# Weaving VectorE's dependent chains in the first pass of a two-layer graph and mixture-of-experts kernel

## The chip, the cores and the metric

The kernel runs on one core of one Trainium2 chip. The metric is the device time of one execution in microseconds, as the median of some runs. A kernel has five engines that matter here: TensorE (PE in the profile, with its weight loads shown as PEld), VectorE (DVE), ScalarE (ACT), GpSimd (POOL) and SyncE (SP). Each runs its own list of instructions in order and waits on semaphores for the others. SP and POOL issue most of the DMAs.

## The reference

There are 128 graphs of 64 nodes with 256 features, 8192 tokens in all, in float32. Two layers follow each other, and each is a graph part and a mixture-of-experts part, with a residual around each of them:

```python
# layer 0
x = x + gnn0(layernorm(x), adj)     # agg = eps*x + adj@x; h = silu(rmsnorm(agg@W1 + b1)); h@W2 + b2
x = x + ffn0(layernorm(x))          # 64 experts, top 6, see below
# layer 1
x = x + gnn1(layernorm(x), adj)     # h = layernorm(x); x + relu((adj@h)@W_rel + b_rel + h@W_root)
x = x + ffn1(layernorm(x))          # 8 experts, top 2, 256 -> 512 -> 256 with relu

def ffn0(x):
    top, idx = top_k(x @ gate_w.T, 6)
    lattice_out = sum_k softmax(top)[k] * (x @ lattice_weights[idx[k]])
    return layernorm(x + lattice_out @ out_w.T + out_b)
```

## The kernel before, in words

The tokens are handled in NB = 32 blocks of C = 256, each of T = 2 tiles of 128 tokens. There are four stretches of work, one after the other.

The first pass (to about 610 us) computes the first graph part and the routing to the 64 experts. It is a software pipeline: `staggered(n, stages)` runs a list of pairs (lag, function), and in step s it calls each function for block s - lag. The list is written by hand, and since PE, DVE and ACT are scheduled by hand, it is also the order of the instructions on these engines. In one step block s gets its hidden layer (`hidden`, 32 matmul records of L716; ScalarE squares them into `sq`, L719), the sum of squares by three halving additions (`square_sum`, L726), the root mean square (`rms`, L730 on TensorE) and the scaling (`scale`: eight times L738 on VectorE and a silu on ScalarE, L740). Block s + 1 gets its statistics and its norm (`norm_a`, L45 and L46; `norm_s`; `norm_b`, L698) and the aggregation over its neighbours (`aggregate`, L706, copied out by ScalarE, L709). Block s - 1 gets the second matrix (`project`, L747 and L749). Block s - 2 gets the residual, its statistics and the layer norm (`residual_a`, `residual_s`, `residual_b`), the transposition (`turn`, L89) and the gate logits (`gate`, L784). Block s - 3 is routed.

Routing is the class `Router`. `choosing` finds the eight largest logits (L217), their indices (L220), and compares the first K = 6 indices with the numbers of the experts (L226), which gives K one-hots per token. `count` multiplies them with a triangle and with ones on TensorE (L240), once for each rank, so that each token gets its position among the tokens of its expert. `placing` adds the running counts (L343 to L354), multiplies with the one-hots (L356) and sums over the experts (L359): the row of each copy of a token in a table in DRAM. `weigh`, `normalize` and `release` make the softmax weights (L306 to L328). `send` writes the six copies of a block's rows to the table by twelve indirect DMAs of GpSimd (L369). `books` are small updates of the chunks of the table's space, in turn over four blocks (`keep_books`). The normed rows go into `xs`, of which there are three buffers; `residual_b` also stores x1 and the normed rows (`xn1_dram`, L771) for the third pass.

The second pass (about 640 to 1150 us) loads the pages of the table in turn, multiplies them with the lattice of their expert, and GpSimd writes the answers back by indirect DMAs (L376).

The third pass (about 1110 to 1520 us) is again a staggered list. It loads the answers (`load_y`), x1 and the normed rows (`load3`, L1107 and L1109), computes the output of the first mixture part (`output`, whose first instruction is L1158, the sum of the projection and the normed rows), the second graph part (L1222 to L1245) and the second routing, with its own `xs` (L1259, three buffers; L315 is GpSimd's write of the destinations into it). Here the VectorE chains are already generators which take turns: `chain` makes from a generator a function that carries it on by one `yield`. Some pages of the second mixture are worked on between the blocks (`up`, L1048, and `down`).

The last stretch runs the pages of the second mixture, L1048 and L1059 on TensorE.

Of the kernel before, what the change touches and what calls it, by code (L numbers as in the profile page):

```python
# [27 lines left out]
class Ops:  # L28
# [55 lines left out]
    def transpose(self, pt, x):  # L84

        n = x.shape[1]
        for k in range(2):
            for t in range(n):
                self.nc.tensor.transpose(pt[:, k, ts(t, P)], x[:, t, ts(k, P)], self.ident)  # L89


class Router:
# [91 lines left out]
    def iota(self, shape, pattern, m, name):  # L184
        t = self.pool.tile(shape, F32, name=self.name + name)
        i = self.small.tile([P, 384], I32, name="iota", bufs=1)[:, :t.free_size()]
        if len(shape) == 3:
            i = i.rearrange("p (a b) -> p a b", b=shape[2])
        self.nc.gpsimd.iota(i, pattern=pattern, base=0, channel_multiplier=m)
        self.nc.vector.tensor_copy(t, i)  # L190
        return t

    def begin(self, counts, work, psum):
# [3 lines left out]
        self.nc.vector.tensor_copy(self.run[:, 0, :], self.base)  # L197

# [12 lines left out]
    def choosing(self, logits, B):  # L211
# [7 lines left out]
        for t in range(T):  # L219
            nc.vector.max_index(idx[:, t, :], top[:, t, :], logits[:, t, :])  # L220
            yield
        which = self.small.tile([P, T, K], F32, name=n + "which")
        nc.vector.tensor_copy(which, idx[:, :, :K])
        yield
        B["hot"] = hot = self.work.tile([P, T, K, E], BF16, name=n + "hot")
        nc.vector.tensor_tensor(hot, self.expert.unsqueeze(1).unsqueeze(1).to_broadcast([P, T, K, E]),  # L226
                                which.unsqueeze(3).to_broadcast([P, T, K, E]), op=ALU.is_equal)
        yield

    def choose(self, logits):  # L230
        B = {}
        for _ in self.choosing(logits, B):
            pass
        return B["top"], B["hot"]

    def count(self, hot):

        for m, lhsT in enumerate((self.tri, self.ones)):
            for k in range(self.K):
                self.nc.tensor.matmul(self.psum[:, m], lhsT=lhsT, rhs=hot[:, :, k, :],  # L240
                                      start=(k == 0), stop=(k == self.K - 1))

    def books(self):
# [5 lines left out]
        def reach_a():  # L249

            v.tensor_tensor(new, run(), self.end, op=ALU.is_ge)
            v.tensor_mul(t, new, self.delta)
            v.tensor_add(run(), run(), t)
            v.tensor_add(self.base, self.base, t)

        def reach_b():
            v.scalar_tensor_tensor(t, new, S, t, op0=ALU.mult, op1=ALU.add)
            v.tensor_add(self.end, self.end, t)
            v.tensor_add(self.none, self.none, new)

        def grow_a():

            v.tensor_sub(t, self.end, run())
            v.scalar_tensor_tensor(new, t, float(self.EP), self.none, op0=ALU.is_lt, op1=ALU.mult)
            v.tensor_tensor_scan(cum, new, self.zero[:, :E], self.used, op0=ALU.add, op1=ALU.add)
            v.tensor_copy(self.used, cum[:, E - 1:E])
            v.tensor_scalar(cum, cum, -1.0, float(self.pitch), op0=ALU.add, op1=ALU.mult)

        def grow_b():
            v.tensor_sub(t, cum, self.end)  # L270
            v.tensor_sub(t, t, self.delta)
            v.tensor_mul(t, t, new)
            v.tensor_add(self.delta, self.delta, t)
            v.tensor_sub(self.none, self.none, new)

        def note_a():

            v.scalar_tensor_tensor(cum, self.alloc, -S, cum, op0=ALU.mult, op1=ALU.add)
            v.tensor_mul(cum, cum, new)

        def note_b():
            self.hit = self.work.tile([P, self.J, E], F32, name=n + "hit", bufs=1)
            v.tensor_tensor(self.hit, self.nth, self.alloc.unsqueeze(1).to_broadcast([P, self.J, E]), op=ALU.is_equal)

        def note_c():
            v.tensor_mul(self.hit, self.hit, cum.unsqueeze(1).to_broadcast([P, self.J, E]))

        def note_d():
            v.tensor_add(self.map, self.map, self.hit)
            v.tensor_add(self.alloc, self.alloc, new)  # L290

        return (reach_a, reach_b), (grow_a, grow_b), (note_a, note_b), (note_c, note_d)

    def keep_books(self, b, half):

        if self.J > 1 and b >= self.epoch:
            if b % self.epoch == 0 and half == 0:
                self.todo = self.books()
            self.todo[b % self.epoch][half]()
# [21 lines left out]
    def normalize(self, w, den):  # L321
        nc = self.nc
        nc.vector.reduce_sum(den, w, axis=AX.X)
        nc.vector.reciprocal(den, den)

# [3 lines left out]

    def places(self, b, hot):  # L330
        B = {"hot": hot}
        for _ in self.placing(B):
            pass
        return B["row"]

    def placing(self, B):
# [13 lines left out]
        if self.J > 1:  # L350
            over = self.work.tile([P, T, E], F32, name=n + "over", bufs=1)
            nc.vector.tensor_tensor(over, place, self.end.unsqueeze(1).to_broadcast([P, T, E]), op=ALU.is_ge)
            nc.vector.tensor_mul(over, over, self.delta.unsqueeze(1).to_broadcast([P, T, E]))
            nc.vector.tensor_add(place, place, over)  # L354
        prod = self.work.tile([P, T, K, E], F32, name=n + "prod", bufs=1)
        nc.vector.tensor_mul(prod, hot, place.unsqueeze(2).to_broadcast([P, T, K, E]))  # L356
# [173 lines left out]
def two_layer_gnn_moe_kernel(ctx: ExitStack, tc: tile.TileContext, a: dict, out: bass.AP):  # L530
# [84 lines left out]
    xn1_dram = [dram.tile([C, D], F32, name=f"xn1_{b}") for b in range(NB)]  # L615
# [21 lines left out]
    with tc.tile_pool(name="c0", bufs=1) as c0, \  # L637
# [23 lines left out]
        nc.scalar.dma_start(out=w1, in_=a["L0_gnn_W1"].rearrange("(k p) f -> p k f", p=P))  # L661
# [23 lines left out]

        def norm_e(b):
# [6 lines left out]
        def norm_b(b):  # L693
# [3 lines left out]
            for t in range(T):  # L697
                nc.vector.tensor_scalar(xn[:, t, :], x[:, t, :], mv[:, t, 0:1], rs[:, t:t + 1],  # L698
                                        op0=ALU.subtract, op1=ALU.mult)

# [21 lines left out]
        def square_sum(b):  # L722
            h = KH
            while h > 1:
                h //= 2
                nc.vector.tensor_add(sq[:, :h, :], sq[:, :h, :], sq[:, h:2 * h, :])  # L726

# [6 lines left out]
        def scale(b):  # L734
# [6 lines left out]
            nc.scalar.preload_act_table_set("natural_log_exp_and_others")  # L741
# [10 lines left out]
        def residual_a(b):  # L752
# [3 lines left out]
            B["mv1"] = ops.stats(x1)  # L756

        def residual_s(b):
            blocks[b]["rs1"] = ops.rstd(blocks[b]["mv1"][:, :, 1], 1e-5)

        def residual_b(b):
            B = blocks[b]
            x1, mv, rs = B["x1"], B["mv1"], B["rs1"]
# [7 lines left out]
            nc.sync.dma_start(out=by_tile(xn1_dram[b]), in_=xs[:, :, 0, :D])  # L771
# [15 lines left out]
        def choose(b):  # L787
            B = blocks[b]
            B["top"], B["hot"] = r0.choose(pg)
# [5 lines left out]
        def count(b):  # L795
            r0.count(blocks[b]["hot"])

        def place(b):
            B = blocks[b]
            r0.normalize(*B["w"])  # L800
            B["row"] = r0.places(b, B["hot"])
# [12 lines left out]
        def load_lattice(b):  # L814
# [10 lines left out]
        norm_b(0)  # L825
# [6 lines left out]
        r0.begin(counts, work, route)  # L832
        staggered(NB, (
            (3, choose),
            (3, lambda b: r0.keep_books(b, 0)),
            (2, residual_a),
            (4, lambda b: send(b, 2)),
            (-2, lambda b: load0(b) if b > 1 else None),
            (-1, rest(norm_a)),
            (0, lambda b: hidden(b, 0)),  # L840
            (0, lambda b: hidden(b, 1)),
            (2, residual_s),
            (-1, rest(norm_s)),
            (-1, rest(norm_e)),
            (4, lambda b: send(b, 3)),
            (3, weigh),
            (0, lambda b: hidden(b, 2)),
            (0, lambda b: hidden(b, 3)),
            (3, count),
            (2, residual_b),  # L850
            (-1, rest(norm_b)),
            (4, lambda b: send(b, 4)),
            (0, split_late),
            (1, lambda b: project(b, 0, 0, 4)),
            (3, lambda b: r0.keep_books(b, 1)),
            (4, lambda b: send(b, 5)),
            (0, square_sum),
# [3 lines left out]
            (2, turn),  # L861
            (0, rms),
            (3, place),
            (1, lambda b: project(b, 1, 0, KH)),
            (2, gate),
            (0, scale),
            (3, lambda b: send(b, 1)),
            (1, load_lattice),
# [170 lines left out]
    def up(i, lo=0, hi=KF):  # L1039
# [5 lines left out]
        for c in range(lo, hi):  # L1045
            ph = Q["ph"](c)
            for k in range(KD):
# [422 lines left out]
```

## Time and profile before

| | |
|---|---|
| runs, us | 2025.9, 2020.5, 2021.36; median 2021.36 |
| the profiled execution's own time, us | 2032.17 |
| its span, us | 2030.3 |
| granted TensorE clock, mean of the span | 0.98 |
| busy share of the span: PE, PEld, DVE, ACT, POOL | 93%, 81%, 58%, 50%, 58% |
| moved by DMA | 397.90 MB, 196 GB/s |

The span is from the first to the last instruction of one profiled execution; its own time is that of the same execution on the device. A row of the timeline has the start in us, the busy time in us, the engine, the line of the kernel, the operation with what it writes and reads, and the number of instructions merged into the row; behind it, in brackets, stands how long the engine sat idle before and what ended that. A row of the groups has the number of instructions, their busy time and the mean of one in ns, and the idle time before them. A row of the waits has who waited for whom, the total in us, how often and the longest.

### The profile page before, as it was taken

The page shows a single profiled execution, that of the slowest core. Times are in us where ns is not written, and L with a number is a line of the kernel's source. Part 1 is how long each engine was busy: PE and PEld are TensorE (multiplying, and loading weights), DVE is VectorE, ACT ScalarE, POOL GpSimd, SP SyncE. Part 2 cuts the span into 40 slices and gives each one's busy share as a digit, 9 for nine tenths or more (in the row PEclk, how much of TensorE's full clock was granted, in tenths as well). Part 3 has the DMA queues.
Part 4 walks back from the last instruction along what each step waited for, and adds up shares of the span by engine and source line. Part 5 has one row for each costly group of instructions (what it writes and reads, how often), then busy time and mean ns, then how long its engine had stood idle before and what let it go on. Part 6 is the DMA issues. An engine that isn't in the chain of part 4 may idle for free. (4 is left out here: it accounts for less than half of the span.)

```text
span 2030.3 us, 36761 instructions
## 1 busy us (share of the span) xinstructions
PE 1898.1 (93%) x10324; PEld 1648.7 (81%) x10324; DVE 1169.2 (58%) x4165; ACT 1012.5 (50%) x2033; POOL 1169.7 (58%) x1134
## 2 busy tenths in 40 slices
PE   6999999999966899999999799999989999999995
PEld 5888888888854777888877588788868888888885
DVE  5899999999975333343333378899852222222221
ACT  4888888888851222222222266666643333333331
POOL 1376667677677777777777734344444444444443
PEclk9999999999977999999999999999999999999998
DMA  4244555544486988766666889988527766766774
GB/s 117 86 143 151 169 166 175 171 157 147 136 264 202 310 259 262 216 206 207 209 208 184 310 311 302 321 305 303 170 89 190 173 162 160 168 157 162 162 162 87
DMA packets 282559, 397.90 MB, mean 196 GB/s; under 512 B 56024, under 2 KB 236392, under 8 KB 282352
## 3 DMA queue, kind: packets, MB, share of 16 engines
q1 hardware_dynamic: 202880, 246.61, 40.8%
q0 software_dynamic: 64416, 136.14, 22.3%
q10 hardware_dynamic: 15056, 12.69, 1.9%
q8 instruction: 93, 1.52, 0.3%
q14 instruction: 114, 0.93, 0.2%
HBM read 222.84 MB, written 176.64 MB: 197 GB/s over the span
## 5 line engine op out<-in xcount | busy, mean ns | idle before, releaser
L369 POOL DMA_INDIRECT r0x<-xs,r0row x384 | 396.5, 1033 | 230.2 <-issue 67.0
L376 POOL DMA_INDIRECT r0y<-px x404 | 393.2, 973 | 124.6 <-DMA r0y<-px 47.3
L974 PE MATMUL py<-lat,pxT 128*128 x1616 | 388.0, 383 | 18.7 <-ACT pxT L961 15.7
L386 POOL DMA_INDIRECT out_x<-py_s,px x138 | 215.3, 1560 | 291.0 <-DMA out_x<-py_s,px 216.2
L978 DVE TENSOR_SCALAR px<-py,px 128x256 f32<-128x256 f32 x404 | 177.0, 480 | 311.4 <-PE py L974 307.5
L974 PEld LDWEIGHTS py<-lat,pxT 128*128 128x128 f32 x1616 | 292.6, 191 | 59.7 <-ACT pxT L961 21.3
L961 ACT COPY pxT<-pt 128x512 f32<-128x512 f32 x202 | 118.1, 586 | 370.4 <-PE pt L959 251.0
L1050 ACT ACTIVATE phid<-ph,pw 128x256 f32<-128x256 f32 x264 | 125.2, 474 | 311.5 <-issue 167.0
L1059 PE MATMUL py<-fw,phid 128*128 (+1 forms) x1072 | 242.5, 379 | 0.1
L1048 PE MATMUL ph<-pxT,pw 128*128 128x256 f32 x1056 | 238.7, 379 | 0.0
L749 PE MATMUL ps<-lat 128*128 128x256 f32 x1024 | 238.5, 381 | 0.0
L716 PE MATMUL ph<-lat 128*128 128x256 f32 x1024 | 233.5, 387 | 2.7 <-DVE lat L738 2.0
L1048 PEld LDWEIGHTS ph<-pxT,pw 128*128 128x128 f32 x1056 | 200.6, 190 | 27.3
L716 PEld LDWEIGHTS ph<-lat 128*128 128x128 f32 x1024 | 196.1, 194 | 29.8 <-issue 2.4
L1059 PEld LDWEIGHTS py<-fw,phid 128*128 128x128 f32 x1072 | 198.5, 190 | 24.6 <-ACT phid L1050 0.3
L749 PEld LDWEIGHTS ps<-lat 128*128 128x128 f32 x1024 | 193.8, 192 | 24.9
L369 POOL DMA_INDIRECT r1x<-xs,r1row x128 | 136.9, 1070 | 76.0 <-ACT hn L1194 14.4
L959 PE MATMUL pt<-ident,px 128*128 128x128 f32 x808 | 126.0, 277 | 13.7 <-DMA px<-r0x 13.3
L1068 DVE TENSOR_SCALAR p<-p 128x2 f32<-128x2 f32 x69 | 11.7, 169 | 219.5 <-ACT p L1067 219.5
L1074 DVE TENSOR_TENSOR py_s<-py,pb 128x512 f32<-128x512 f32 x67 | 46.4, 692 | 152.6 <-PE py L1059 152.6
L959 PEld LDWEIGHTS pt<-ident,px 128*128 128x128 f32 x808 | 100.9, 142 | 40.1 <-issue 10.0
L719 ACT ACTIVATE lat<-ph,c_L_gnn_b 128x256 f32<-128x256 f32 x256 | 103.5, 471 | 13.6 <-PE ph L716 11.9
(322 smaller groups left out, 2951.1 us busy)
## 6 DMA issues: line engine op xcount, KB each, us to landing
px<-r0x SPq DMA_DIRECT2D x404, 129.0 KB
y<-r0y SPq DMA_DIRECT2D x64, 768.0 KB
pw<-in_L_ffn_W1b SPq DMA_DIRECT2D x69, 514.0 KB
px<-r1x SPq DMA_DIRECT2D x69, 258.0 KB
x<-x SPq DMA_DIRECT2D x64, 256.0 KB
pb<-in_L_ffn_b SPq DMA_DIRECT2D x69, 128.0 KB
r0x<-r0filler ACTq DMA_DIRECT2D x64, 129.0 KB
lat<-in_x SPq DMA_DIRECT2D x32, 256.0 KB
```

The lines of the kernel that those rows point to most:

```text
L369: i = self.nc.gpsimd.indirect_dma_start(out=self.table[:, :], out_offset=bass.IndirectOffsetOnAxis(ap=row[:, t, k:k + 1], axis=0), in_=xs[ ...
L376: d = self.nc.gpsimd.indirect_dma_start(out=self.answer[:, :], out_offset=bass.IndirectOffsetOnAxis(ap=x[:, self.D:self.D + 1].bitcast(I32 ...
L386: i, d = f"{self.name}add{i}", self.nc.gpsimd.indirect_dma_start(out=self.total[:, :], out_offset=bass.IndirectOffsetOnAxis(ap=x[:, self.D ...
L716: nc.tensor.matmul(ph[:, c, :], lhsT=w1[:, k, ts(2 * j + c, P)], rhs=B["aggT"][:, k, :], start=(k == 0), stop=(k == KD - 1))
L749: nc.tensor.matmul(B["po"][:, t, :], lhsT=B["hT"][:, c, ts(t, P)], rhs=w2[:, c, :], start=False, stop=(t == T - 1 and c == KH - 1))
L959: nc.tensor.transpose(pt[:, k, ts(q, P)], Q["px"][:, q, ts(k, P)], ident)
L961: nc.scalar.copy(xT[:, :, :n * P], pt[:, :, :n * P])
L974: nc.tensor.matmul(py[:, q, :], lhsT=xT[:, k, ts(q, P)], rhs=lat[:, ds(regs["e"][(2 * j + q) % 4], 1), k, :].rearrange("p o d -> p (o d)") ...
L978: nc.vector.tensor_scalar(px[:, q, :D], py[:, q, :], px[:, q, D + 1:D + 2], None, op0=ALU.mult)
L1048: nc.tensor.matmul(ph, lhsT=w[:, k * F1 + c * P:k * F1 + (c + 1) * P], rhs=Q["xT"][:, k, :], start=(k == 0), stop=(k == KD - 1))
L1050: nc.scalar.activation(hid[:, c, :], ph, AF.Relu, bias=w[:, KD * F1 + c:KD * F1 + c + 1], scale=1.0)
L1059: nc.tensor.matmul(py[:, t, :], lhsT=Q["hid"][:, c, ts(t, P)], rhs=fw2[:, ds(e, 1), c, :].rearrange("p o d -> p (o d)"), start=(c == 0), s ...
```

## The change

The first pass's list is written anew, with finer pieces. The generators of the third pass come to the first: `chain` becomes a function of its own, and `choosing`, `residual_a`, `square_sum`, `normalize`, `placing`, `scale`, the norm's parts and the books now yield behind each VectorE instruction, so that one chain's instruction stands between two of another. The six count matmuls on each of the two weights become one, on a sum of the six one-hots. The one-hots are compared as bf16 tensors, with the rank as the innermost dimension. The normed rows are not stored; the third pass computes them from x1 and the kept factor `rs1`, leaving the mean to the layer norm that follows. W1 is loaded by SP's queue in place of ScalarE's, behind the first block. The third pass gets a fourth `xs` buffer, and `up` there computes the chunks in pairs. The diff, cut to its core:

```diff
+def chain(blocks, make, key=None):
+    key = key or make.__name__
+    def advance(b, n=1):
+        B = blocks[b]
+        if key not in B:
+            B[key] = make(b)
+        for _ in range(n):
+            if next(B[key], B) is B:
+                break
+    return advance
...
+        self.tags = work.tile([P, self.E, self.K], BF16, name=self.name + "tags", bufs=1)
+        self.nc.vector.tensor_copy(self.tags, self.expert.unsqueeze(2).to_broadcast([P, self.E, self.K]))
...
-        which = self.small.tile([P, T, K], F32, name=n + "which")
+        which = self.small.tile([P, T, K], BF16, name=n + "which")
...
-        B["hot"] = hot = self.work.tile([P, T, K, E], BF16, name=n + "hot")
-        nc.vector.tensor_tensor(hot, self.expert.unsqueeze(1).unsqueeze(1).to_broadcast([P, T, K, E]),
-                                which.unsqueeze(3).to_broadcast([P, T, K, E]), op=ALU.is_equal)
+        B["hot"] = hot = self.work.tile([P, T, E, K], BF16, name=n + "hot", bufs=1 if K > 2 else 2)
+        nc.vector.tensor_tensor(hot, self.tags.unsqueeze(1).to_broadcast([P, T, E, K]),
+                                which.unsqueeze(2).to_broadcast([P, T, E, K]), op=ALU.is_equal)
+        B["marks"] = [hot[:, :, :, k] for k in range(K)]
...
+        if K > 2:
+            marks = self.work.tile([P, T, E], BF16, name=n + "marks")
+            B["marks"] = [marks]
+            with nc.allow_low_precision("a token's experts differ: each sum is 0 or 1"):
+                nc.vector.tensor_reduce(marks, hot, op=ALU.add, axis=AX.X)
+            yield
+
+    def count(self, marks):
         for m, lhsT in enumerate((self.tri, self.ones)):
-            for k in range(self.K):
-                self.nc.tensor.matmul(self.psum[:, m], lhsT=lhsT, rhs=hot[:, :, k, :],
-                                      start=(k == 0), stop=(k == self.K - 1))
+            for k, rhs in enumerate(marks):
+                self.nc.tensor.matmul(self.psum[:, m], lhsT=lhsT, rhs=rhs, start=(k == 0), stop=(k == len(marks) - 1))
...
-        nc.vector.tensor_mul(prod, hot, place.unsqueeze(2).to_broadcast([P, T, K, E]))
+        nc.vector.tensor_mul(prod, hot.rearrange("p t e k -> p t k e"), place.unsqueeze(2).to_broadcast([P, T, K, E]))
...
-    xn1_dram = [dram.tile([C, D], F32, name=f"xn1_{b}") for b in range(NB)]
+    rs1 = const.tile([P, NB, T], F32, name="rs1")
...
-        nc.scalar.dma_start(out=w1, in_=a["L0_gnn_W1"].rearrange("(k p) f -> p k f", p=P))
+        nc.sync.dma_start(out=w1, in_=a["L0_gnn_W1"].rearrange("(k p) f -> p k f", p=P))
...
-            nc.sync.dma_start(out=by_tile(xn1_dram[b]), in_=xs[:, :, 0, :D])
...
+        H, R, Q, V, S, Y = (chain(blocks, f) for f in (choose, residual_a, square_sum, normalize, slots, scale))
+        M, X = (rest(chain(blocks, f)) for f in (norm_n, norm_b))
+        L, U = (chain(blocks, lambda b, half=half: r0.keep_books(b, half), ("books", half)) for half in range(2))
         staggered(NB, (
-            (3, choose),
...
+            (0, lambda b: hidden(b, 0)),
+            (0, lambda b: hidden(b, 1)),
+            (2, R),
+            (-2, lambda b: load0(b) if b > 1 else None),
+            (3, H),
+            (2, R),
+            (3, H),
...
+            (2, residual_s),
+            (3, weigh),
+            (-1, M),
+            (3, H),
...
+            (3, count),
             (-1, rest(aggregate)),
             (-1, load_late),
             (1, lambda b: project(b, 0, 4, KH)),
             (2, turn),
+            (3, S),
+            (0, Q),
+            (3, S),
+            (0, Q),
+            (4, lambda b: send(b, 5)),
             (0, rms),
+            (3, S),
+            (3, S),
+            (3, S),
+            (3, S),
+            (3, S),
             (1, lambda b: project(b, 1, 0, KH)),
             (2, gate),
-            (0, scale),
+            (0, Y),
+            (3, S),
+            (0, Y),
+            (3, S),
+            (0, Y),
+            (3, place),
+            (0, Y),
...
@@ up
-        for c in range(lo, hi):
-            ph = Q["ph"](c)
...
+        for c0 in range(lo, hi, Q["group"]):
+            group = range(c0, c0 + Q["group"])
+            ph = [Q["ph"](c) for c in group]
...
@@ load3 and output
-            B["xn1"] = xn1 = work.tile([P, T, D], F32, name="xn1", bufs=3)
-            nc.sync.dma_start(out=xn1, in_=by_tile(xn1_dram[b]))
...
-            nc.vector.tensor_add(h, B["pp"], B["xn1"])
-            yield
+            for t in range(T):
+                nc.vector.scalar_tensor_tensor(h[:, t, :], B["x1"][:, t, :], rs1[:, b, t:t + 1], B["pp"][:, t, :],
+                                               op0=ALU.mult, op1=ALU.add)
+                yield
...
@@ residual of the third pass
-            B["xs"] = xs = work.tile([P, T, 2, W], F32, name="xs", bufs=3)
+            B["xs"] = xs = work.tile([P, T, 2, W], F32, name="xs", bufs=4)
```

## The prediction

> **What bounds the kernel now.** I read the page first: TensorE is busy 93% of the span, and the slices of section 2 show three passes, with a first one (slices 1 to 11) in which VectorE is as full as TensorE. The change touches that pass most, so I read its windows next. The columns are the busy time of PE, PEld, DVE, ACT and POOL, then the clock granted to TensorE, the DMA share and GB/s.
>
> ```profile
> 100.00:300.00 200.00, 199.04 (x1129) 175.84 (x1129) 189.19 (x649) 171.54 (x331) 139.09 (x136) 1.00 0.48 158
> ```
>
> TensorE shows 99.5%, VectorE 94.6%. Which of them sets the step? The ends of matmuls are modelled, so a busy TensorE proves little; the timeline, start against start, does. One L730 runs per block.
>
> ```profile
> 94.62 0.60 PE L730 MATMUL rms_p<-lat,mean 128*128 128x256 f32 x2
> 111.98 0.60 PE L730 MATMUL rms_p<-lat,mean 128*128 128x256 f32 x2
> 129.34 0.60 PE L730 MATMUL rms_p<-lat,mean 128*128 128x256 f32 x2
> ...
> 317.51 0.50 PE L240 MATMUL route<-r0hot,r0tri 128*128 128x128 bf16 x6
> 317.84 0.50 PE L240 MATMUL route<-r0hot,r0ones 128*128 128x128 bf16 x6
> 318.18 0.38 PE L747 MATMUL ps<-p_L_gnn_b,r0ones 128*128 128x512 bf16 x1
> ...
> 554.06 0.60 PE L730 MATMUL rms_p<-lat,mean 128*128 128x256 f32 x2
> ```
>
> Before the bookkeeping starts a step is 17.36 us, twice running: TensorE's own pace. From 129.34 to 554.06 it is 424.72 us for 24 steps, 17.70 each, so something else holds it. VectorE's timeline tells what:
>
> ```profile
> 302.08 2.40 DVE L726 TENSOR_TENSOR lat<-lat 128x1024 f32<-128x1024 f32 x3
> ...
> 308.54 3.22 DVE L738 SCALAR_TENSOR_TENSOR lat<-ph,c_L_gnn_b,rms 128x256 f32<-128x256 f32 x8
> ```
>
> The eight L738 last 475 ns each but take 3.22 us together: independent neighbours overlap by 83 ns (8 x 475 less 7 x 83). The three L726 (1224, 692 and 425 ns, each needing the one before) take 2.40 us for 2.34 us of work: a dependent one waits some 34 ns more. So a dependent neighbour costs 117 ns more than an independent one. A step has about 56 VectorE instructions of together 19.84 us (the groups of 100 to 540 us, by step); in 22 pairs the second needs the first. 19.84 - 34.6 x 0.083 + 21.75 x 0.034 = 17.71 us. That is the step: VectorE bounds it, with TensorE 0.35 us behind.
>
> **The first pass.** The costliest VectorE groups of the routing (busy us, mean ns | idle before):
>
> ```profile
> L738 DVE SCALAR_TENSOR_TENSOR lat<-ph,c_L_gnn_b,rms 128x256 f32<-128x256 f32 x195 | 78.5, 475 | 0.0
> L226 DVE TENSOR_TENSOR r0hot<-r0expert,r0which 128x768 bf16<-128x768 f32 x25 | 24.0, 958 | 0.9
> L356 DVE TENSOR_TENSOR r0prod<-r0hot,r0place 128x768 f32<-128x768 bf16 x25 | 23.9, 958 | 0.9
> L359 DVE TENSOR_REDUCE r0rowf<-r0prod 128x12 f32<-128x768 f32 x25 | 23.8, 953 | 0.9
> ```
>
> *Counts.* 12 matmuls L240 become 2. They take 318.18 - 317.51 = 0.67 us, so 10 of 12 are 0.56 us, and TensorE's own step is 17.36 - 0.56 = 16.80 us. The multi-hot sum is a new VectorE reduction over 768 elements; its nearest row is L359, +0.95 us (0.9 to 1.5: its 128 rows of 6 are shorter than L359's 12 rows of 64).
>
> *One-hots in bf16.* No row shows a bf16 compare of two tensors, so 958 ns is the upper end. [...] Sum and compare together still cost 0.55 us more than before: by themselves they would make the step 18.26 us.
>
> *L356 now reads the one-hots at steps of 12 bytes.* [...] No row here has such an operand in a long instruction. [...] I take 0, [...]and keep 0.80 for the range.
>
> *Weave.* In the new order 6 of 57 pairs are dependent, not 22: the five slot steps (L348 to L356) stay in a row, while scale, row reduction, statistics, squares and books alternate. 20.25 - 51 x 0.083 + 6.25 x 0.034 = 16.2 us of VectorE per step (20.25 is 19.84 plus 0.95 less 0.40, and rounding). [...] The two timeline rows above differ by 117 ns a pair, and a sum made with it meets the measured step to 0.01 us; I go by them.
>
> *What is late next.* TensorE 16.80, VectorE 16.2 (17.0 in the step with reach_a and reach_b). ScalarE is busy 171.54 us in 200, 15.1 per step, but one chain of it matters: last hidden matmul, two squares (0.8), the two xs activations (3.2), the aggT copy (0.6), then the transposes of turn. That is 4.7 us; TensorE's own work over the same stretch was 5.2 us and becomes 4.7 without the ten matmuls. The slack is gone, so I add 0.1. With the longer reach step now and then I take 16.93 us.
> Gain: 24 x (17.70 - 16.93) = 18.5 us; the four steps from 59 to 129 us 4 x 0.45 = 1.8; the last full one 0.4.
>
> *End of the pass.* It is paced by GpSimd's sends, and what follows waits for the last:
>
> ```profile
> 573.25 0.97 POOL L369 DMA_INDIRECT r0x<-xs,r0row  x1 [0.30 <-DVE r0rowf L359]
> 639.03 0.97 POOL L369 DMA_INDIRECT r0x<-xs,r0row  x1 [0.30 <-issue]
> 641.57 10.87 SPq L515 DMA_DIRECT2D px<-r0x  x16
> ```
>
> Fifty sends stand there at about 1.3 us. The reduction adds 0.55 us to each drain step on VectorE, but those are 12.6 us apart and the sends of a block take 15.3: GpSimd covers it. If that cover goes, it is 4 x 0.6 us. In steady state twelve sends at 1.27 us from start to start, 15.2 us, still fit into 16.9. So the gain reaches the second pass whole (I allow 1.5 us either way). That pass has GpSimd's replies back to back (234 in 300 us) and is not touched.
>
> *W1 on SP's queue*, behind x and the adjacency of block 0, and ahead of block 1's x, W2 and the small loads:
>
> ```profile
> 8.64 0.43 DVE L688 TENSOR_TENSOR at<-at,eye 128x256 f32<-128x256 f32 x1 [2.09 <-DMA at<-in_adjT]
> ...
> 12.19 9.86 PE L716 MATMUL ph<-lat 128*128 128x256 f32 x32 [0.68 <-ACT lat L709]
> ```
>
> W1 (1 MB) shared the engines with these; without it the adjacency can land before its wait and hidden can start up to 3 us earlier, unless W1, issued 1.5 us later, is then late. Ends -3 and +1; I take -2. Block 1's norm waits for ScalarE's squares, not for its loads.
>
> **Third pass.** Undisturbed steps are 10.21 us, without TensorE idle (1380 to 1460); between 1230 and 1372 steps of up to 12.7 us add 10.3 us. What waits there:
>
> ```profile
> POOL xs L315 <- DMA r1x<-xs,r1row: 51.1, 11, 7.0
> ACT xs L1259 <- DMA r1x<-xs,r1row: 19.8, 7, 4.3
> ...
> 1274.01 0.33 PE L89 MATMUL ps<-ident,xs 128*128 128x128 f32 x1 [1.48 <-ACT xs L1259]
> ```
>
> ScalarE can't write xs until the sends of three blocks earlier have landed, with DMA at 0.9 to 1.0 of its time. A fourth xs buffer gives 10 us more, against a longest wait of 4.3; dropping xn1 takes 32 x 256 KB of writes (pass 1) and as many reads here, 12% of what a block loads. I take 6 of the 10.3 us (0 to 10). The sum h as two instructions of some 475 ns, not one of 680, adds 0.19 us to VectorE, which waits 0.6 us for the counts (L343) in every step. Pairs in up(): at most 0.5 us, where three blocks' pages are interleaved. From 1521 us TensorE runs back to back through the expert pages: all of it reaches the end.
>
> **Sum.** 18.5 + 1.8 + 0.4 + 2 + 6 = 28.7, less a little for the drain: 28 us of the profiled execution's 2032.17 (span 2030.3), so 2004. That execution lies 10.8 us above the median of the runs, 2021.36; from the median it is 1993 us.
>
> **The rivals.**
> *VectorE stays the bound* (14%): reads at 12 bytes or short rows cost 0.4 to 1.1 us. Then 17.2 us a step: 24 x 0.5 + 2 + 6 = 20 less drain, 2003, to 2008 at 17.4. For it: no row has such an operand[...].
> *All cover holds* (8%): steps of 16.8, 10 us in pass 3, 3 at the start: 37 us, 1984.
> *No change* (4%): a new in-order wait, VectorE's L765 on ScalarE's rstd, closes a loop silu, table load, squares, rstd, L765, slots, scale. By durations it is 16.6 us; near 17.9, with 0.3 us of pass 3, nothing is left: 2018 to 2024. Against it: rstd is asked for earlier in the new order.
> *Slower* (7%): the layout with the expert outside and the rank inside stalls its users: [...] 16.2 + 3.1 = 19.3 us a step, 24 x 1.6 = 38 us lost, less 8: 2051. It decides from a VectorE step of 18.3 us on, 2.1 over mine; then the losses pass the 8 us of start and third pass by the 6 us (0.3%) that a measurement of this kernel can tell from no change.
> That the counts don't do what they say is excluded: each mark is 0 or 1, and both matmuls use it.
>
> **How the numbers follow.** My forecast has 67%, and its own range is 1985 to 2001. With the first two rivals the range of 8 in 10 is 1981 to 2008. Faster by over 0.3% (below 2015): 67 + 14 + 8 = 0.89; within: 0.04; slower: 0.07.
>
> **What would show it.** L730 to L730 near 16.9 us in place of 17.70; the bf16 compare at 557 ns and the sum at 950; L356 still at 958; GpSimd's last send of the pass some 22 us earlier; the waits of xs for r1x gone. Wrong: steps above 17.3, a compare at 958, or steps over 11 us in the third pass.

## The result and the profile after

The changed kernel took 2002.37 us (median of 6 runs, 1998.95 to 2006.5) and the kernel before 2024.41 us on the same chip (6 runs, 2020.5 to 2029.59): a ratio of 0.9885, with a 95% interval of 0.9869 to 0.9900. A later measurement gave 2004.44 against 2028.47 us, ratio 0.9883 (0.9859 to 0.9907). So 22 to 24 us are gained, where 28 were forecast. The profiled execution took 2002.07 us (span 2000.2), 30.1 us less than that of the kernel before. The marks that cut both traces into stretches are the row of the mean square (L730 before, L774 after, one per block), the last send of the first pass, and the last graph convolution of each block in the third pass (L1239 and L1325):

| stretch of the profiled execution | before, us | after, us | difference |
|---|---|---|---|
| start to first mean square | 26.36 | 23.70 | -2.7 |
| first to 32nd mean square | 544.16 | 521.35 | -22.8 |
| to the last send of the first pass | 68.51 | 68.58 | +0.1 |
| to the first convolution of the third pass | 526.0 | 522.4 | -3.6 |
| first to last convolution (third pass) | 328.8 | 316.4 | -12.4 |
| to the end | 536.5 | 547.8 | +11.3 |

The windows of the changed kernel, with the columns as before: TensorE has no idle time left in the first pass by its modelled ends, and ScalarE has gone from 171.54 to 179.00 us in 200.

```profile
100.00:300.00 200.00, 200.00 (x1059) 175.72 (x1058) 189.20 (x682) 179.00 (x344) 142.57 (x143) 1.00 0.46 147
```

The timeline has the mean square of block 7 and that of the last block:

```profile
141.04 0.60 PE L774 MATMUL rms_p<-lat,mean 128*128 128x256 f32 x2
...
545.05 0.60 PE L774 MATMUL rms_p<-lat,mean 128*128 128x256 f32 x2
```

That is 404.01 us for 24 steps. All of them are 16.85 to 16.87 us but the last, 16.27; the steps with the longer bookkeeping no longer stand out. VectorE's timeline shows the weave. The three halving additions L769 need each other, and between them stand two instructions of the routing:

```profile
154.36 1.22 DVE L769 TENSOR_TENSOR lat<-lat 128x1024 f32<-128x1024 f32 x1
155.50 0.22 DVE L379 TENSOR_TENSOR r0run<-r0run,route 128x64 f32<-128x64 f32 x1
155.63 0.69 DVE L769 TENSOR_TENSOR lat<-lat 128x512 f32<-128x512 f32 x1
156.23 0.21 DVE L381 TENSOR_TENSOR r0run<-r0run,route 128x64 f32<-128x64 f32 x1
156.36 0.42 DVE L769 TENSOR_TENSOR lat<-lat 128x256 f32<-128x256 f32 x1
...
157.09 0.29 DVE L388 TENSOR_TENSOR r0over<-r0place,r0endrow 128x128 f32<-128x128 f32 x1
157.41 0.29 DVE L390 TENSOR_TENSOR r0over<-r0over,r0delta 128x128 f32<-128x128 f32 x1
157.74 0.29 DVE L392 TENSOR_TENSOR r0place<-r0place,r0over 128x128 f32<-128x128 f32 x1
```

The second to fifth of these start 0.08 to 0.09 us before the end of the one in front of them. The last three need each other and stand in a row: L390 and L392 start 0.03 to 0.04 us after it. These are the two prices of the prediction (83 ns less and 34 ns more), side by side in one step. Counted over 24 steps of each trace, an average step of the kernel before has 36 instructions that start before the end of the one in front (by 80 ns on average) and 21 that start just after it (36 ns). In the changed kernel these are 52 and 5, and VectorE stands idle for another 0.95 us a step, where it was 0.1 us before.

The costliest groups of the routing, from 100 to 540 us (busy us, mean ns | idle before):

```profile
L395 DVE TENSOR_TENSOR r0prod<-r0hot,r0place 128x768 f32<-128x768 bf16 x26 | 31.7, 1219 | 0.9
L251 DVE TENSOR_REDUCE r0marks<-r0hot 128x128 bf16<-128x768 bf16 x27 | 25.5, 944 | 0.0
L398 DVE TENSOR_REDUCE r0rowf<-r0prod 128x12 f32<-128x768 f32 x26 | 24.5, 942 | 0.0
L243 DVE TENSOR_TENSOR r0hot<-r0tags,r0which 128x768 bf16<-128x768 bf16 x27 | 14.2, 525 | 0.0
```

The compare fell from 958 to 525 ns, the sum costs 944 ns, and the product L395, which reads the one-hots at steps of 12 bytes, rose from 958 to 1219 ns.

The first pass's last send of GpSimd stood at 639.03 us and is now 25.4 us earlier:

```profile
613.63 0.97 POOL L408 DMA_INDIRECT r0x<-xs,r0row  x1 [0.30 <-issue]
```

The end of the kernel looks different. These are the shares of the chain that ended last, first before the change, then after it. TensorE had it alone; now the DMA of the out_x adds has a large part of it:

```profile
PE 24%; DMA 0%; issue 0%; ACT 0%; POOL 0%; DVE 0%; POOLq 0%; ACTq 0%
```

```profile
PE 12%; DMA 9%; POOL 3%; issue 2%; DVE 1%; ACT 0%; POOLq 0%; SPq 0%; DVEq 0%; ACTq 0%
```

And the waits from 1500 to 1960 us (who waited for whom, total us, times, longest) have two entries that the kernel before doesn't have at all, the third and the fourth of these. The first is of the kernel before, the others are of the changed one:

```profile
POOL out_x L386 <- DMA out_x<-py_s,px: 184.8, 47, 4.7
```

```profile
POOL out_x L425 <- DMA out_x<-py_s,px: 238.4, 58, 5.8
...
DVE py_s L1172 <- DMA out_x<-py_s,px: 57.5, 19, 5.3
...
PE pt L89 <- DMA px<-r1x: 8.7, 12, 2.4
```

From the start of one page's first L1157 to that of the next, TensorE took 7.35 us for nearly every page before. After, 28 of the pages took longer; what they took above 7.35 us, from the third page on, comes to 16.6 us in all (0.3 us before). I call this sum TensorE's excess. One such page in the timelines of GpSimd, SP and TensorE:

```profile
1644.76 1.55 POOL L425 DMA_INDIRECT out_x<-py_s,px  x1 [0.30 <-issue]
1652.13 1.55 POOL L425 DMA_INDIRECT out_x<-py_s,px  x1 [5.82 <-DMA out_x<-py_s,px]
```

```profile
1651.51 0.38 SPq L554 DMA_DIRECT2D px<-r1x  x1
```

```profile
1654.34 0.63 PE L89 MATMUL pt<-ident,px 128*128 128x128 f32 x4 [1.02 <-DMA px<-r1x]
```

GpSimd waited 5.82 us behind the issue of a page's second add until it had landed (about 4 is usual). When it lands, SP issues the load of the page four further on, which had been waiting for the px buffer, and 0.62 us later the next page's add starts. TensorE stands idle for 1.02 us until the load is there. Experiments 3 to 12 follow this up.

### The profile page after: what moved, and what is told of

Its sections match the earlier page's. It is cut to its first block, busy times and chain, and to the rows that moved or that the text cites. A ratio compares the mean times of both kernels' runs of the same rounds, so it can differ in the third digit from the quotient of the medians.

```text
span 2000.2 us, 36067 instructions
## 1 busy us (share of the span) xinstructions
PE 1879.9 (94%) x10004; PEld 1628.7 (81%) x10004; DVE 1150.2 (58%) x4231; ACT 1010.0 (50%) x2033; POOL 1160.2 (58%) x1134
## 5 line engine op out<-in xcount | busy, mean ns | idle before, releaser
L408 POOL DMA_INDIRECT r0x<-xs,r0row x384 | 386.9, 1008 | 216.9 <-ACT lat L784 114.3
L1157 PE MATMUL py<-fw,phid 128*128 (+1 forms) x1072 | 243.2, 380 | 1.3 <-issue 0.6
L1157 PEld LDWEIGHTS py<-fw,phid 128*128 128x128 f32 x1072 | 198.5, 190 | 27.7 <-issue 2.3
L1172 DVE TENSOR_TENSOR py_s<-py,pb 128x512 f32<-128x512 f32 x67 | 46.3, 691 | 173.3 <-PE py L1157 101.4
L782 DVE SCALAR_TENSOR_TENSOR lat<-ph,c_L_gnn_b,rms 128x256 f32<-128x256 f32 x256 | 111.9, 476 | 23.2 <-ACT rms L72 23.2
```

The source lines that it names most:

```text
L408: i = self.nc.gpsimd.indirect_dma_start(out=self.table[:, :], out_offset=bass.IndirectOffsetOnAxis(ap=row[:, t, k:k + 1], axis=0), in_=xs[ ...
L1157: nc.tensor.matmul(py[:, t, :], lhsT=Q["hid"][:, c, ts(t, P)], rhs=fw2[:, ds(e, 1), c, :].rearrange("p o d -> p (o d)"), start=(c == 0), s ...
```

## The experiments

Times are medians; the ratio is against runs of the kernel before that were made beside them. Of each edit the core is shown.

**1. The new counts without the weave.**

```diff
 (the kernel before)
+        hot = work.tile([P, T, E, K], BF16) ; marks = tensor_reduce(hot)
-        12 count matmuls
+        2 count matmuls
```

> The kernel before with the new counts alone (bf16 one-hots with the rank innermost, their sum, two count matmuls in place of twelve), in the old order of instructions. Theory of the pairs (a VectorE instruction costs 83 ns less than its duration behind an independent one, 34 ns more behind one that it needs): VectorE's step of 17.71 us gets the sum (0.94 us and 0.03 for its dependence), 0.43 less for the compare and 0.26 more for the strided product: 18.5 us a step from 130 to 550 us, 24 x 0.8 = 19 us slower than before in the first pass, ratio near 1.009. Rival, that TensorE sets the step: its ten matmuls less give 16.8 to 16.9 us and 20 us gained, ratio 0.99.

2056.0 against 2028.73 us, ratio 1.0141 (1.0114 to 1.0168). The mean square in the timeline:

```profile
148.56 0.60 PE L738 MATMUL rms_p<-lat,mean 128*128 128x256 f32 x2
...
575.92 0.60 PE L738 MATMUL rms_p<-lat,mean 128*128 128x256 f32 x2
```

427.36 us for 23 steps, 18.58 each, against 18.5 expected. TensorE has ten matmuls less per block and is no faster for it: the theory that TensorE set the step falls. Alone, this half of the change loses 0.88 us a step against the kernel before. From here to the changed kernel only the order (with the smaller edits) differs, and a step goes from 18.58 to 16.86 us. The medians differ by 27 us, where 19 were expected. By the traces the first pass is 23.9 us longer up to its last send: 21 in the 24 steps, and the rest in the steps before them (17.7 us, where TensorE had set 17.36) and in a drain 1.7 us longer.

**2. The weave without the new counts.**

```diff
 (the changed kernel)
-        hot = work.tile([P, T, E, K], BF16) ; marks = tensor_reduce(hot)
+        hot = work.tile([P, T, K, E], BF16) ; no marks, which in float32
-        2 count matmuls
+        12 count matmuls
```

> The changed kernel with the old counts (float one-hots with the expert innermost, no sum, twelve count matmuls), in the new order. Theory of the pairs: VectorE falls to about 16 us a step, TensorE's own 17.36 us sets it with 0.05 to 0.1 on top, so 17.4 to 17.5 us, 26 x 0.55 = 14 us more than the changed kernel in the first pass, and 6 to 8 us less than the kernel before there. [...] VectorE keeps its 17.7 us a step, nothing gained over the kernel before in that pass. Elsewhere as the changed kernel: whole time about 2016 us by the first, 2022 by the second.

2012.97 us, ratio 0.9932 (0.9907 to 0.9956).

```profile
143.89 0.60 PE L766 MATMUL rms_p<-lat,mean 128*128 128x256 f32 x2
...
544.38 0.60 PE L766 MATMUL rms_p<-lat,mean 128*128 128x256 f32 x2
```

23 steps in 400.49 us, 17.41 each: TensorE's own 17.36 and 0.05 on top, as expected. The rival theory, that the order buys nothing and VectorE keeps its 17.7 us, falls. The last send of the first pass stands at 629.8 us, 16.2 us behind the changed kernel's (14 were expected) and 9.2 ahead of the kernel before (6 to 8). So the order alone takes 0.3 us a step, the counts alone cost 0.9, and together they bring 0.8: the weave makes room on VectorE, and the counts then shorten TensorE. The whole is some 10 us behind the changed kernel, less than the pass is, since the last stretch was shorter here (535.1 us against 547.8).

**3. The normed rows stored and loaded again.**

```diff
+            nc.sync.dma_start(out=by_tile(xn1_dram[b]), in_=xs[:, :, 0, :D])
+            nc.sync.dma_start(out=xn1, in_=by_tile(xn1_dram[b]))
-                nc.vector.scalar_tensor_tensor(h[:, t, :], x1, rs1, pp, ...)
+            nc.vector.tensor_add(h, B["pp"], B["xn1"])
```

> The changed kernel, but the normed rows are stored in the first pass and loaded in the third again (h as one sum), with the fourth xs buffer kept. In the profile the third pass of the changed kernel has steps of 10.21 us throughout. Theory of the buffer: the fourth buffer took the waits away, so the third pass stays within 2 us of the changed kernel. Theory of the traffic: with 16 MB more the sends land late again, steps of 11 us and more come back, 5 to 12 us longer. For the last stretch, where the changed kernel loses 11 us to late landings of the out_x adds (7.5 us a page for 7.35): if the place of the tables in DRAM, which moves with the 8 MB of normed rows, is the cause, a page is back at 7.35 us here; if it is not, it stays at 7.4 to 7.5.

**4. Three xs buffers in the third pass.**

```diff
-            B["xs"] = xs = work.tile([P, T, 2, W], F32, name="xs", bufs=4)
+            B["xs"] = xs = work.tile([P, T, 2, W], F32, name="xs", bufs=3)
```

> The changed kernel with three xs buffers in the third pass in place of four, normed rows not stored. Theory of the buffer: ScalarE and GpSimd wait for the sends of three blocks earlier again, some steps of 11 to 12 us, 5 to 10 us longer in the third pass. Theory of the traffic: with the normed rows gone the sends land in time, the steps stay at 10.21 us, no more than 2 us lost. Together with the run that keeps the rows this tells which of the two took the 12.4 us.

The rows kept: 2000.61 us, ratio 0.9861 (0.9831 to 0.9891), third pass 316.1 us. Three buffers: 2005.79 us, ratio 0.9888 (0.9860 to 0.9915), third pass 321.7 us. The changed kernel's third pass was 316.4 us and, in a second profile (experiment 9), 318.1. The waits of the run with three buffers, from 1160 to 1440 us:

```profile
POOL xs L355 <- DMA r1x<-xs,r1row: 8.5, 2, 5.3
...
ACT xs L1345 <- DMA r1x<-xs,r1row: 2.9, 1, 2.9
```

In the changed kernel the first of these is 0.2 us and the second is absent. In the kernel of experiment 1, which has three buffers and moves the rows, ScalarE's wait comes to 16.3 us in the same window, in 6 times.

With four buffers the 16 MB of rows show no effect in the third pass (316.1 us for 316.4). With three they probably do. What the steps of this pass, from the fifth to the 28th, took above 10.21 us comes to 10.3 us in the kernel before and 6.7 in experiment 1, which both have three buffers and the rows, to 4.1 with three buffers and no rows, and to 0.4 in the changed kernel. So once the rows are gone the fourth buffer is worth 3.7 us, between the two theories' 5 to 10 and 2 at most. How much of the rest was the rows' is not shown: these are single profiles, and experiment 1 also lacks the pairs of `up`. The changed kernel's 316.4 and 318.1 us differ in the step before the last (9.90 and 11.57 us), which has no part in this. As to the last stretch, a page from add to add is 7.45 us with the rows kept: their place in DRAM is not the cause.

**5 to 8: the last stretch and the start.** These four ran on a chip on which their mean granted clock was 0.92 to 0.93 and the kernel before took 2284.42 us, at 0.94 to 0.95. The first two passes are so much longer there that the totals say nothing on a few us; I read the third pass and the last stretch, where the clock was 1.00 but for the passage between them (0.93 in run 6), and come back to that chip at the end.

```diff
 5: -  pages[i].update(..., ph=half, group=2, ...)
    +  pages[i].update(..., ph=half, group=1, ...)
```

> The changed kernel with the chunks of the third pass's first expert pages computed singly again (group 1 in place of 2). Theory of the adds: from the second page on the chain of GpSimd's out_x adds (each page waits until the page before has landed) sets the end of the kernel, at first add + 68 cycles + 14 us; the pairs only brought TensorE 3 to 4 us closer to it, so without them the backlog of the adds starts near 6 us in place of 8.4, TensorE's page steps above 7.4 us all but vanish (excess below 4 us in place of 16.6), and the whole time stays within 3 us of the changed kernel. Theory of TensorE: it sets the end, and the 8 waits of 0.56 us in the kernel before come back, 4 us longer.

```diff
 6: -  name="px", bufs=4 ; py_s and p with 2
    +  name="px", bufs=6 ; py_s and p with 4
```

> The changed kernel with four py_s buffers in place of two, six px in place of four and four p, so that TensorE can run two pages farther ahead of the adds. Theory of the adds (their chain sets the end): TensorE's excess over 7.35 us a page goes to below 2 us, the backlog of the adds grows to 15 us and more, and the whole time stays within 3 us of the changed kernel. Theory of jitter (single late landings pass through two buffers to TensorE, which sets the end): with more buffers the adds catch up, and 8 to 14 us are gained.

```diff
 7: the first page's answer
    +            (4, ahead((-2, lambda: share(-4)), (-2, lambda: answer(-4)))),   # behind count1
    -        share(-4) ; answer(-4)   # behind page_table
```

> The changed kernel with the first page's answer (its share, sum and two out_x adds) moved in front of the last block's four r1x sends on GpSimd, 8 us earlier. Theory of the adds: their chain starts earlier and the second page's adds stand 4 to 5 us earlier, which come off the end whole: 3 to 5 us less than the changed kernel, with the same cycle. Theory of TensorE: the last sends land 3.7 us later, the first pages behind them are fetched later, nothing gained and up to 3 us lost.

```diff
 8: -  nc.sync.dma_start(out=w1, ...)
    +  nc.scalar.dma_start(out=w1, ...)
```

> The changed kernel with W1 loaded by ScalarE's queue again. If sharing the engines with the adjacency of block 0 is what W1 cost: hidden starts near 12.2 us in place of 10.25, the first row of the mean square stands at 26.0 to 26.5 us in place of 23.7, 2 to 2.7 us longer. If the earlier start came from the new order of the norm's parts: hidden stays near 10.3 us and nothing is lost.

| run | time, us | ratio (interval) | last convolution to end, us | TensorE's excess, us | backlog of the adds at the third page, us |
|---|---|---|---|---|---|
| 5, chunks singly | 2331.98 | 1.0209 (1.0167 to 1.0250) | 543.1 | 7.3 | 7.2 |
| 6, deep buffers | 2313.89 | 1.0156 (1.0117 to 1.0194) | 536.2 | 0 | 14.9 |
| 7, add early | 2320.61 | 1.0135 (1.0089 to 1.0180) | 539.1 | 6.5 | 5.4 |
| 8, W1 on ScalarE's queue | 2326.83 | 1.0138 (1.0079 to 1.0198) | 545.8 | 12.2 | 8.6 |

The backlog is the time from a page's sum on VectorE (L1172) to its first add on GpSimd; it was 5.9 us in the kernel before and 8.4 in the changed one. Run 6 decides between the theories: with more buffers the excess is gone, the stretch is 9.6 us shorter than in run 8, and the backlog, 14.9 us at the start, falls to 8.8. My theory that the adds' own chain sets the end expected no gain, and falls. In run 7 the stretch is 6.7 us shorter than in run 8, and run 5 missed its numbers: the backlog started at 7.2 and not near 6, and the excess was 7.3 and not below 4. But of the excess of these two little can be read. The kernels of experiments 2 and 4 have the last stretch of the changed kernel unaltered, and their excess was 5.7 and 7.6 us, so one profile of each can't tell 6.5 or 7.3 from it. Run 8 gave the start:

```profile
12.25 8.72 PE L759 MATMUL ph<-lat 128*128 128x256 f32 x32 [0.68 <-ACT lat L752]
```

The hidden layer starts at 12.25 us, against 9.70 to 10.62 in the eleven profiles with W1 on SP's queue: 1.6 to 2.5 us are W1's. The expected 26.0 for the first mean square was 25.28 (23.63 to 24.79 in the other three runs of that chip).

**9 to 12: which buffer.** These ran on a chip on which the kernel before took 2028.47 us.

> The changed kernel once more, for the spread of its last stretch. If the late landings are a trait of the changed kernel and not of one execution: 69 pages at 7.40 to 7.53 us from add to add, TensorE's excess over 7.35 us a page 7 to 17 us in all, backlog of the adds at the third page above 8 us. If they were an accident: below 7.37 us a page, excess under 3 us.

> The changed kernel with four py_s and four p in place of two, px kept at four. Theory that VectorE's wait for a free py_s hands the late landings to TensorE (62 us of such waits in the changed kernel): most of TensorE's excess goes, below 6 us, what is left waits for px, and 4 to 8 us are gained. Rival, that a free px is what is late (the load of page i + 4 waits for the adds of page i): excess stays at 7 us or more, nothing gained.

> The changed kernel with six px in place of four, py_s and p kept at two. Theory of py_s: excess stays at 7 to 17 us, nothing gained (within 3 us). Rival (px is late): excess below 6 us, 4 to 8 us gained.

> The changed kernel with both: four py_s and p, six px, and the first page's answer in front of the last four r1x sends. In the run with the deep buffers TensorE had no excess left and the stretch from the third pass's last step to the end took 536 us in place of 548. Expected: excess 0, and 10 to 14 us less than the changed kernel in the same job. If the adds' own chain is the limit once the buffers are there, the earlier start brings another 3 to 5 us of it; if TensorE is, it brings nothing beyond the buffers.

Run 9 has no edit. Run 10 has the py_s and p of run 6, run 11 its px, and run 12 is run 6 and run 7 in one.

| run | time, us | ratio (interval) | last convolution to end, us | TensorE's excess, us |
|---|---|---|---|---|
| 9, changed kernel again | 2004.44 | 0.9883 (0.9859 to 0.9907) | 544.5 | 11.4 |
| 10, four py_s | 2005.76 | 0.9884 (0.9858 to 0.9909) | 547.3 | 13.6 |
| 11, six px | 1996.23 | 0.9850 (0.9822 to 0.9877) | 535.7 | 0 |
| 12, both, add early | 1992.66 | 0.9830 (0.9805 to 0.9854) | 536.2 | 0 |

Run 9 says that the waits are a trait of the changed kernel, though their sum differs from profile to profile. With four py_s the wait of VectorE is gone, and that of TensorE stays; this is run 10, from 1480 to 1960 us:

```profile
PE pt L89 <- DMA px<-r1x: 6.5, 6, 2.7
```

So VectorE's 57 us of waits for a free py_s cost nothing. What cost was px: four buffers, of which the load of page i + 4 gets the one of page i when the adds of page i have landed. With six (run 11) TensorE is never idle, and the median is 8 us lower than in run 9. The windows from 1480 to 1960 us, first of run 11, then of the changed kernel:

```profile
1480.00:1960.00 480.00, 480.00 (x2356) 422.77 (x2355) 118.01 (x331) 170.49 (x396) 201.98 (x130) 1.00 0.71 166
```

```profile
1480.00:1960.00 480.00, 469.38 (x2273) 406.57 (x2272) 108.91 (x317) 163.54 (x378) 197.19 (x127) 1.00 0.68 162
```

Run 12, with the early add and the four py_s on top, has the same stretch to half a us, so these two bring nothing that the intervals can tell. In run 11 the adds still end last, from 1829 us on, level with TensorE; in run 12 TensorE has the chain that ended last, as in the kernel before:

```profile
PE 25%; DMA 0%; POOL 0%; issue 0%; DVE 0%; ACT 0%; ACTq 0%; POOLq 0%
```

Run 12 beats both kernels, by 36 us and by 12.

## Why the prediction was right, and where it was off

*The first pass.* Right in its mechanism: VectorE's chain got out of the way, and TensorE's own work became the limit, at 16.86 us a step. That the number, 16.93, was so near is luck. I had put 0.1 us on top of TensorE's 16.80 for a chain of ScalarE and something for the longer bookkeeping. Neither shows: TensorE has no idle time in the step, and all steps are alike. The 0.06 us stand in the eight matmuls of the aggregation, first of the kernel before, then of the changed one:

```profile
108.92 1.05 PE L706 MATMUL ps<-at,lat 128*128 128x128 f32 x8
109.81 1.89 PE L749 MATMUL ps<-lat 128*128 128x256 f32 x8
```

```profile
137.92 1.11 PE L749 MATMUL ps<-at,lat 128*128 128x128 f32 x8
138.87 1.89 PE L795 MATMUL ps<-lat 128*128 128x256 f32 x8
```

From their start to that of the next matmul it is 0.95 us for 0.89. In the new order they stand right behind the counts. In experiment 2, with twelve counts in front, it is 0.95 us too, which is its 17.41 for 17.36. VectorE's 16.2 us holds a slip (19.84 plus 0.95 less 0.40 is 20.39 and not 20.25, so 16.4); the trace has 15.9, that is 16.86 less 0.95 of idle time. Over the 24 steps of the prediction's sum this is 424.72 less 404.6, that is 20.1 us for 18.5.

*The price of a pair.* The 117 ns came from two rows of one trace, and they held: in the changed kernel an instruction behind an independent one starts 0.08 to 0.09 us before its end, as the eight L738 did (0.083). The step was 16.86 us, with one VectorE instruction more, and the same counts in the old order made it 18.58. Here the order of independent instructions was worth at least 1.7 us a step, since TensorE is the limit at 16.86.

*One-hots and sum.* The compare took 525 ns for 557 (558 in experiment 1), the sum 944 for 950. That the compare would give back 0.40 us was an estimate of mine, which no row of the kernel before showed; it gave 0.43 (0.40 in experiment 1), and sum and compare together cost 0.51 us for 0.55. The product at 12-byte steps was mis-sized: 0.26 us and not 0, inside the bounds of 0 and 0.80. The upper bound was an estimate too: another 1.04 ns for each of 768 elements, which is what L726 takes for an element more (425, 692 and 1224 ns for 256, 512 and 1024). In the old order also the product takes 958 ns with dense one-hots and 1226 at 12-byte steps (experiment 1), so the layout is the cause. It costs nothing in this kernel, as VectorE waits 0.6 us a step for ScalarE's root (16.0 us in 25 waits from 100 to 540 us). The rise is a third of a ns per element (261 ns for 768). The 3.1 us that the rival "slower" put on product, compare and sum rested on no row; the three took 0.22 us more than forecast (2688 ns for 2465).

*End of the pass and W1.* Carried whole, as forecast: 68.58 us for 68.51. The start gave 2.7 us for 2, and 1.6 to 2.5 of it are W1's.

*Third pass: 12.4 us for 6, above the bound of 10.* The mechanism was right: the waits of xs are gone, the fourth buffer alone is worth 3.7 us, and the rows had at most a part in it as long as there were three. The size was met in a usual run: experiment 1, with the old buffers and rows, took 323.9 us for this stretch and not 328.8, and 318.1 was more usual for the changed kernel than 316.4. The pairs in `up`, put at 0.5 us at most, were mis-sized: the last step is 9.63 us without them (the kernel before, experiments 1 and 5) and 8.29 with them, 1.3 us. The spread of this stretch also explains in part why the profiled executions differ by 30.1 us and the medians by 22 to 24.

*The last stretch: +11.3 us for 0. This step failed.* The prediction said: "From 1521 us TensorE runs back to back through the expert pages: all of it reaches the end." It read TensorE's full rows and did not ask how far away the next limit was. GpSimd's adds need as long for a page as TensorE's 7.35 us: two issues of 1.85 and 1.55 us and a mean wait of 3.91 us before a page's first add make 7.3. In the changed kernel that wait is 4.10 us (4.02 in experiment 9); 0.18 us more, 68 times, are 12 us. And with four px buffers TensorE has to wait too, as each late landing delays the load of a page.

Over the profiles with four px the excess goes with this mean: it was 0.3 to 5.7 us at 3.91 to 3.92 (the kernel before, experiments 1 and 2), 6.5 to 12.2 at 3.96 to 4.02 (experiments 3 to 5 and 7 to 9), 13.6 and 16.6 at 4.06 and 4.10 (experiment 10, and the changed kernel's first profile). With six px it was 0, at 3.88 to 3.93. Why the adds land later in most kernels with the new order, and sooner again with six px, is open. A lack of room at the start of the stretch is not enough to explain it. The changed kernel's first add stands 1.3 us ahead of the third page's matmuls L1157 (1474.61 and 1475.95), where it stood 4.8 us ahead before (1516.51 and 1521.26). But experiment 2 had 1.4 us and an excess of 5.7, and experiment 5, without the pairs, had 3.9 us and an excess of 7.3.

*The total.* 28 us were forecast from the profiled execution, and 22 to 24 measured between medians: the first pass and the start brought 25, the second pass's 3.6 is within its spread (522.4 to 528.2 us in the profiles of one clock), the third pass some 6 of its 12 in a usual run, and the last stretch took 8 to 11 back. That the total lies near the forecast from the profile is luck in part: the first pass and the start gave some 2.7 us more than the sum had for them, which covers a part of a loss that the sum did not have.

## What to carry to other kernels

When two engines have nearly the same step, price both before shortening one: here the edit for TensorE lost 0.88 us a step without the one for VectorE, and VectorE's alone brought 0.3 of the 0.84 that the two brought together. VectorE's step was a sum over neighbours here, and putting another chain's instruction between two that need each other was worth 117 ns a pair (83 ns of overlap and 34 ns of wait). Behind every stretch that seems to run back to back, look for the chain with the same period, and count the buffers that tie its landing to the next load. Here two more px buffers took the waits away.

## What the runs showed of the hardware that was not expected

The indirect DMAs that add into out_x in DRAM landed unevenly: the time that GpSimd waited for a page's two adds was mostly 3.4 to 4.6 us (58 of 68 waits in the kernel before, 52 in the changed one), with single waits of 5 to 6.7 us in the changed kernel (4.7 at most in the kernel before). A mean of 4.0 in place of 3.9, 68 times, is worth as much as a change of the kernel.

On the chip of experiments 5 to 8 the granted clock fell to half within the first two passes, again and again: in run 6 the mean of every 50 us up to 1450 us is 0.65 to 0.97. These are windows of that run (the columns as before, the clock third from the end) and a row of its timeline:

```profile
302.00:304.00 2.00, 0.35 (x1) 0.00 (x0) 2.00 (x5) 2.00 (x2) 0.00 (x0) 0.50 0.15 33
304.00:306.00 2.00, 0.61 (x3) 0.61 (x4) 1.86 (x7) 1.34 (x2) 1.14 (x2) 0.50 0.00 0
306.00:308.00 2.00, 2.00 (x7) 1.65 (x6) 0.77 (x1) 1.15 (x3) 1.59 (x1) 0.50 0.18 66
```

```profile
300.14 1.62 ACT L762 ACTIVATE lat<-ph,c_L_gnn_b 128x256 f32<-128x256 f32 x4 [6.06 <-remote]
```

ScalarE waits 6.06 us for a hidden layer whose matmuls are all issued and, by the modelled ends, done: it looks as if TensorE itself stood still, and it went on at half clock for some 10 us (the clock was 1.00 up to 300 us, and again from 312 to 330 us). The step from the mean square at 306.30 us to that at 325.89 us is 19.6 us long, and from 100 to 700 us, with a clock of 0.89 to 0.91, TensorE gets through 770 to 809 matmuls in 200 us, where the changed kernel's first profile has 1059. From 1500 to 1700 us, in the third pass, the clock of this run is 1.00. No run shows what stopped TensorE, nor why it went on at half clock. All four kernels, near kin of the changed one, were 1.4 to 2.1% slower there than the kernel before. So the gain of this change is shown on chips where the mean granted clock was 0.97 to 0.98, and not on this one, at 0.92 to 0.93; whether fuller use of TensorE brings the pauses was not tried.
